# B's rows copied to four blocks of 32 partitions, B spread by 32-row matmuls, and one projection bank for two batches in a Mamba kernel

## The chip, the cores and the metric

The kernel runs on one core of a Trainium2 chip. The metric is the time of one execution on the device in microseconds (us); of several executions the median is taken. TensorE is called PE, VectorE DVE, ScalarE ACT, GpSimd POOL and the queue that issues most DMAs SP, as in the profile.

## What is computed

Four layers run one after the other on x of shape (4, 96, 64, 64). Layers 0 and 2 are the same block with two Mamba sublayers each; layer 1 is a state-space layer of another kind, and layer 3 a ConvNeXt block. Only layers 0 and 2 are touched. One Mamba sublayer, cut to what matters:

```
h   = layernorm(seq)                          # (B, L=4096, C=96)
xs, z = split(h @ in_w)                       # 192 channels each
xc  = silu(causal_conv4(xs) + conv_b)
dbl = xc @ xproj_w                            # 6 + 16 + 16 columns
dt, Bm, Cm = dbl[:6], dbl[6:22], dbl[22:38]
delta = softplus(dt @ dt_w + dt_b)            # 192 channels
dA  = exp(delta * A)                          # 192 channels x 16 states
dBx = delta * Bm * xc
hs[t] = dA[t] * hs[t-1] + dBx[t]              # a scan over L
y   = (sum over states of hs * Cm + D * xc) * silu(z)
seq = seq + y @ out_w
```

Bm and Cm are the same for all 192 channels, so each of their rows has to be brought to every channel's partition.

## The kernel before, in words

The activations X stay on chip as 96 partitions x 4 batches x 4096 positions. `mamba_fusion` runs a Mamba layer in 32 steps: 2 pairs of batches x 2 sublayers x 8 tiles of T = 512 positions. In a step both batches of a pair are worked on: 2 x 192 channels fill three tiles j of 128 partitions (`SEGS`): j = 0 holds 128 channels of the first batch, j = 1 the last 64 of the first batch and the first 64 of the second, j = 2 the other 128 of the second. Two layers make 64 steps.

A step has a front and a scan. `mamba_front` (L141) is a generator: layernorm of both batches, the projections pu (with the convolution folded in, L165) and pz (L173), a SiLU on ACT between two loads of its function table, then pd (L189), which is `xproj` and gives dt, a row of ones (added by the bias `one7`), B and C as 39 rows for each batch. Each batch has its own pd bank and eviction into `dbl[b]` (L193), and C is written to DRAM from there (L194). Then pt (L202) makes delta from 7 rows of `dbl`, and ACT, DVE and POOL finish the softplus (delta, du).

`mamba_scan` (L214) walks through 24 groups of GS = 2 states (8 groups for each j). For a group it does the following. `spread` multiplies a selector `sel` with `dbl[b]` on PE, which puts B's row s on all partitions of a two-bank PSUM tile bs (L232); the selector and `dbl` have 128 rows, of which one counts. A DMA brings C's rows to all partitions (cs, L259). ACT makes da (L262, recorded at L96). DVE multiplies bs by du (L263) and runs two scans (L268). POOL multiplies hs by cs (L269), and PE sums over states with an identity (py, L246). The spread of group n + 1 is issued before the scans of group n, the sums of group n - 1 after them. bs has two buffers, so spread n + 1 waits until the scans of group n - 1 have read theirs.

The next step's front is woven in by hand: after each group one `next()` takes one more piece of the front, up to its next `yield`. There are 15 pieces, so groups 0 to 14 of a step have front work behind them and the later ones don't. The order on each engine comes from the framework's scheduler, which follows this program order but may let ready work pass. In j = 1 a spread has two matmuls of 64 columns for each state, one for each batch.

Of the kernel before, what the change touches and what calls it, by code (L numbers as in the profile page):

```python
# [16 lines left out]
F32 = mybir.dt.float32  # L17
AF = mybir.ActivationFunctionType
ALU = mybir.AluOpType
# [6 lines left out]
P = 128  # L26
T = 512
# [6 lines left out]
DIN = 192  # L34
NST = 16
RANK = 6
NXP = RANK + 1 + 2 * NST
GS = 2


# [97 lines left out]
    nc.gpsimd.tensor_tensor(relu, relu, w, ALU.add)  # L138


def mamba_front(tc, k, X, pools, wt, pair, c, h2, dbl4, made):  # L141

    nc = tc.nc
    work, psum, dram = pools
    h, hprev = h2[c % 2], h2[(c + 1) % 2]
    if c == 0:
        nc.vector.memset(h[:C, :, 0:3], 0.0)
    else:
        nc.vector.tensor_copy(h[:C, :, 0:3], hprev[:C, :, T : T + 3])
    for b in range(2):  # L150
        layernorm(
            nc, k, (work, psum), X[:, 2 * pair + b, ds(c * T, T)], h[:C, b, 3 : 3 + T],
            wt["ln"][:, 0:1], wt["ln"][:, 1:2], tag="mm",
        )
        yield

    xz = made["xz"] = work.tile([P, 6, T], F32, name="xz", bufs=2)
    for j in range(3):  # L160
        pu = psum.tile([P, T], F32, tag="mm", name="pu")
        for r0, r1, d0, d1, b in SEGS[j]:
            for tap in range(4):
                kk = C + 1 if tap == 3 else C
                nc.tensor.matmul(  # L165
                    pu[r0:r1], lhsT=wt["conv"][:kk, tap, d0:d1], rhs=h[:kk, b, ds(tap, T)],
                    start=(tap == 0), stop=(tap == 3),
                )
            yield
        nc.scalar.copy(xz[:, j], pu)  # L170
        pz = psum.tile([P, T], F32, tag="mm", name="pz")
        for r0, r1, d0, d1, b in SEGS[j]:
            nc.tensor.matmul(  # L173
                pz[r0:r1], lhsT=wt["in"][:, DIN + d0 : DIN + d1], rhs=h[:C, b, 3 : 3 + T],
                start=True, stop=True,
            )
        nc.scalar.copy(xz[:, 3 + j], pz)
        yield
    k.act.other(xz, xz, AF.Silu)
    yield  # L180

    cd = made["cd"] = dram.tile([2, NST, T], F32, name="cd")
    dbl = made["dbl"] = dbl4[c % 2]
    for b in range(2):
        pd = psum.tile([P, T], F32, tag="mm", name="pd")[:NXP]
        for n, (j, r0, r1) in enumerate(ROWS[b]):
            nc.tensor.matmul(  # L189
                pd, lhsT=wt["xproj"][r0:r1, j], rhs=xz[r0:r1, j], start=(n == 0), stop=(n == 1)  # L190
            )
        db = dbl[b]
        nc.scalar.activation(db[:NXP], pd, AF.Identity, bias=wt["one"])  # L193
        nc.sync.dma_start(cd[b], db[RANK + 1 + NST : NXP])  # L194
        yield

    delta = made["delta"] = work.tile([P, 3, T], F32, name="delta", bufs=2)
    du = made["du"] = work.tile([P, 3, T], F32, name="du", bufs=2)
    for j in range(3):
        pt = psum.tile([P, T], F32, tag="mm", name="pt")  # L200
        for r0, r1, d0, d1, b in SEGS[j]:
            nc.tensor.matmul(  # L202
                pt[r0:r1], lhsT=wt["dt"][:, d0:d1], rhs=dbl[b][: RANK + 1], start=True, stop=True
            )
        ua = work.tile([P, T], F32, name="ua")
        lg = work.tile([P, T], F32, name="lg")
        nc.scalar.activation(ua, pt, AF.Abs)
        nc.vector.tensor_scalar_max(delta[:, j], pt, 0.0)
        softplus_tail(nc, k.act, delta[:, j], ua, lg, du[:, j])
        nc.gpsimd.tensor_tensor(du[:, j], delta[:, j], xz[:, j], ALU.mult)  # L210
        yield


def mamba_scan(tc, k, X, pools, wt, sel, pair, c, carry, made, fuse):  # L214

    nc = tc.nc
    state, psum = pools
    xz, cd, dbl, delta, du = made["xz"], made["cd"], made["dbl"], made["delta"], made["du"]
    groups = [(j, s0) for j in range(3) for s0 in range(0, NST, GS)]

    def spread(n):

        j, s0 = groups[n]
        bs = psum.tile([P, GS, T], F32, tag="bs", name="bs", bufs=2)
        for s in range(GS):  # L230
            for r0, r1, _, _, b in SEGS[j]:
                nc.tensor.matmul(  # L232
                    bs[r0:r1, s], lhsT=sel[:, s0 + s, r0:r1], rhs=dbl[b], start=True, stop=True
                )
        return bs

    def close(j, py):
        nc.vector.scalar_tensor_tensor(
            xz[:, j], xz[:, j], wt["d"][:, j : j + 1], py, ALU.mult, ALU.add
        )  # L240
        nc.gpsimd.tensor_tensor(xz[:, j], xz[:, j], xz[:, 3 + j], ALU.mult)

    def sums(n, py, hc):
        j, s0 = groups[n]
        for s in range(GS):
            nc.tensor.matmul(  # L246
                py, lhsT=k.ident, rhs=hc[:, s], start=(s0 + s == 0), stop=(s0 + s == NST - 1)
            )
        if s0 + GS == NST:
            close(j, py)  # L250

    bs = spread(0)
    last = None
    for n, (j, s0) in enumerate(groups):
        if s0 == 0:
            py = psum.tile([P, T], F32, tag="py", name="py", bufs=2)
        cs = state.tile([P, GS, T], F32, name="cs", bufs=4)
        for r0, r1, _, _, b in SEGS[j]:
            nc.sync.dma_start(cs[r0:r1], cd[b, s0 : s0 + GS, :].partition_broadcast(r1 - r0))  # L259
        da = state.tile([P, GS, T], F32, name="da", bufs=3)  # L260
        for s in range(GS):
            k.act.exp_ln(da[:, s], delta[:, j], AF.Exp, scale=wt["a"][:, j, s0 + s : s0 + s + 1])  # L262
        nc.vector.tensor_tensor(bs, bs, du[:, j : j + 1].to_broadcast([P, GS, T]), ALU.mult)  # L263
        ahead = spread(n + 1) if n + 1 < len(groups) else None
        hs = state.tile([P, GS, T], F32, name="hs", bufs=3)
        for s in range(GS):
            init = 0.0 if c == 0 else carry[:, j, s0 + s : s0 + s + 1]
            nc.vector.tensor_tensor_scan(hs[:, s], da[:, s], bs[:, s], init, ALU.mult, ALU.add)  # L268
        nc.gpsimd.tensor_tensor(cs, hs, cs, ALU.mult)  # L269
        if c < NT - 1:  # L270
            nc.scalar.copy(carry[:, j, s0 : s0 + GS], hs[:, :, T - 1])  # L271
        if last is not None:
            sums(*last)
        last = (n, py, cs)
        bs = ahead
        yield
    sums(*last)

    for b in range(2):
        po = psum.tile([P, T], F32, tag="mm", name="po")[:C]  # L280
        for n, (j, r0, r1) in enumerate(ROWS[b]):
            nc.tensor.matmul(
                po, lhsT=wt["out"][r0:r1, j], rhs=xz[r0:r1, j], start=(n == 0), stop=(n == 1)
            )
        xs = X[:, 2 * pair + b, ds(c * T, T)]
        nc.vector.tensor_tensor(xs, xs, po, ALU.add)
        fuse(2 * pair + b, c)


def mamba_weights(nc, act, wpool, w, sub, one7):  # L290
    wt = {"one": one7}
    for name, shape in (
        ("ln", [C, 2]), ("in", [C, 2 * DIN]), ("xproj", [P, 3, NXP]), ("dt", [RANK + 1, DIN]),
        ("a", [P, 3, NST]), ("d", [P, 3]), ("out", [P, 3, C]),
    ):
        wt[name] = wpool.tile(shape, F32, name=f"w_{name}{sub}")
        nc.sync.dma_start(wt[name], w[name][sub])
    conv = wt["conv"] = wpool.tile([C + 1, 4, DIN], F32, name=f"w_conv{sub}")
    nc.sync.dma_start(conv[:C], w["conv_wT"][sub].partition_broadcast(C))
    nc.sync.dma_start(conv[C : C + 1, 3], w["conv_b"][sub : sub + 1])  # L300
# [9 lines left out]
def mamba_fusion(ctx: ExitStack, tc, k, X, res, w):  # L310
# [17 lines left out]
    for b in range(B):  # L328
# [7 lines left out]
    gb = one.tile([C, B], F32, name="gb")  # L336
    nc.scalar.activation(gb, pg2, AF.Identity, bias=vec[:, 1:2])

    one7 = one.tile([NXP, 1], F32, name="one7")
    nc.gpsimd.memset(one7, 0.0)  # L340
    nc.gpsimd.affine_select(
        out=one7, in_=one7, compare_op=ALU.not_equal, fill=1.0, base=-RANK,
        pattern=[[0, 1]], channel_multiplier=1,
    )
    h2 = [one.tile([C + 1, 2, T + 3], F32, name=f"h{i}") for i in range(2)]
    for h in h2:
        nc.vector.memset(h[C : C + 1], 1.0)

    sel = one.tile([P, NST, P], F32, name="sel")
    nc.gpsimd.memset(sel, 0.0)  # L350
    nc.gpsimd.affine_select(
        out=sel, in_=sel, compare_op=ALU.not_equal, fill=1.0, base=-(RANK + 1),
        pattern=[[-1, NST], [0, P]], channel_multiplier=1,
    )
    dbl4 = [[one.tile([P, T], F32, name=f"dbl{i}{b}") for b in range(2)] for i in range(2)]
    for db in dbl4[0] + dbl4[1]:
        nc.gpsimd.memset(db, 0.0)
    stats = one.tile([C, B * NT, nc.vector.BN_STATS_DIM], F32, name="stats")

    def fuse(b, c):  # L360
# [10 lines left out]
    def front(n, made):  # L371
        if n < len(steps):
            pair, sub, c = steps[n]
            yield from mamba_front(tc, k, X, (work, psum, dram), wts[sub], pair, c, h2, dbl4, made)


    made = {}
# [565 lines left out]
```

## Time and profile before

| what | value |
|---|---|
| median of 3 runs | 13629.11 us (13625.45 to 13630.94) |
| profiled execution, its own time | 13637.25 us |
| its span in the profile | 13635.5 us |
| mean granted PE clock | 0.978 |
| L232 spread, PE records | 8192, 3031.1 us busy |
| L246 sums over states, PE records | 6144, 2994.9 us busy |
| L268 scans, DVE | 2688 with a carry, 3304.5 us busy |
| L263 bs times du, DVE | 1536, 1873.7 us busy |
| L269 hs times cs, POOL | 1536, 3620.2 us busy |

An fp32 matmul leaves two records on PE, each with its weight load on PEld. Busy times are unions of spans, and the spans of neighbouring PE records overlap, so PE is read best by the distance from one start to the next. In an answer in order of time the columns are the start, the length, the engine, the line, the operation, output and inputs, rows * columns of the array, shapes, the count of merged instructions, and in brackets the idle time before with what ended it. Of the chain of work that ended last, 60% of the span lies on PE and 24% on DVE.

### The profile page before, as it was taken

To read this page: it belongs to the slowest core of one execution; us is meant where nothing else is said; L and a number is where in the kernel's file an instruction comes from. 1 tells how busy PE (TensorE), PEld (TensorE's weight loads), DVE (VectorE), ACT (ScalarE), POOL (GpSimd) and SP (SyncE) were. 2 spreads that over 40 slices of the span, in tenths; PEclk is the share of its full clock that TensorE was granted. 3 is DMA by queue.
4 is the path that set the end of the run, shared out by engine and by line. 5 is a ranking of instruction groups with operands and counts; after the bars stand their busy time and mean duration, and the time that the engine had idled before them with its cause. 6 is when DMAs were issued, how large, how long until landed. Compare 5 with 4: busy or idle time off the path is not lost.

```text
span 13635.5 us, 125211 instructions
## 1 busy us (share of the span) xinstructions
PE 12543.4 (92%) x43016; PEld 5819.2 (43%) x43016; DVE 9062.4 (66%) x11224; ACT 5552.3 (41%) x9606; POOL 6819.1 (50%) x4814
## 2 busy tenths in 40 slices
PE   8999999999997999999999999899999999999887
PEld 2333333333334666666666666333333333333232
DVE  6777777777775444444444444677777777777798
ACT  3444444344443444444444444444444434444233
POOL 4555555555553444444444344555555555555344
PEclk9999999999998999999999999999999999999887
DMA  3333333333332000000000000233333333333100
GB/s 104 95 98 100 95 98 98 98 101 95 98 99 60 1 1 5 1 1 5 1 1 1 5 1 1 90 95 99 100 94 99 97 98 101 97 98 100 57 8 9
DMA packets 248125, 853.46 MB, mean 63 GB/s; under 512 B 40065, under 2 KB 41345, under 8 KB 246722
## 3 DMA queue, kind: packets, MB, share of 16 engines
q1 hardware_dynamic: 247490, 845.47, 20.4%
q8 instruction: 341, 5.59, 0.2%
q14 instruction: 294, 2.41, 0.1%
HBM read 828.54 MB, written 16.78 MB: 62 GB/s over the span
## 4 chain that ended last, share of the span: by engine, by line
PE 60%; DVE 24%; issue 6%; POOL 6%; ACT 4%; DMA 1%; DVEq 0%; POOLq 0%; SPq 0%; ACTq 0%
DVE hs L268 14%; PE front L558 14%; PE bs L232 11%; PE py L246 10%; PE pu L165 7%; DVE bs L263 6%; PE att L603 2%; PE y L640 2%; POOL y L837 2%; PE y L644 2%; PE out L680 1%; PE out L684 1%; POOL cs L269 1%; PE pz L173 1%; DVE acc L811 1%
## 5 line engine op out<-in xcount | busy, mean ns | idle before, releaser
L269 POOL TENSOR_TENSOR cs<-hs,cs 128x1024 f32<-128x1024 f32 x1536 | 3620.2, 2358 | 2948.9 <-DVE hs L268 2125.6
L246 PE MATMUL py<-cs,ident 128*128 128x512 f32 x6144 | 2994.9, 610 | 426.0 <-POOL cs L269 420.3
L268 DVE TENSOR_TENSOR_SCAN hs<-da,carry,bs 128x512 f32<-128x512 f32 x2688 | 3304.5, 1266 | 123.5 <-ACT da L96 2.4
L232 PE MATMUL bs<-dbl,sel 128*128 128x512 f32 (+1 forms) x8192 | 3031.1, 603 | 141.9 <-DVE hs L268 141.9
L263 DVE TENSOR_TENSOR bs<-bs,du 128x1024 f32<-128x1024 f32 x1536 | 1873.7, 1220 | 1233.3 <-PE bs L232 1233.2
L96 ACT ACTIVATE da<-delta,w_a 128x512 f32<-128x512 f32 x3072 | 2053.9, 712 | 314.8 <-DVE hs L268 312.5
L246 PEld LDWEIGHTS py<-cs,ident 128*128 128x128 f32 x6144 | 1078.7, 189 | 2234.4 <-issue 1201.0
L232 PEld LDWEIGHTS bs<-dbl,sel 128*128 128x128 f32 (+1 forms) x8192 | 1022.9, 163 | 1930.8 <-issue 1532.4
L558 PE MATMUL front<-sconv,xn 96*128 96x320 f32 (+1 forms) x4096 | 1215.5, 436 | 4.7 <-DVE pre L570 4.7
L271 ACT COPY carry<-hs 128x2 f32<-128x2 f32 x1344 | 257.6, 192 | 2174.1 <-DVE hs L268 2174.0
L626 POOL TENSOR_TENSOR ce<-ce,pre 128x384 f32<-128x384 f32 x496 | 509.5, 1027 | 974.9 <-ACT ce L96 974.1
L610 DVE TENSOR_SCALAR seg<-att,dac 128x128 f32<-128x128 f32 x1536 | 452.6, 343 | 744.7 <-PE att L607 733.6
L165 PE MATMUL pu<-h,w_conv 96*128 96x512 f32 (+3 forms) x2048 | 934.9, 601 | 6.8 <-ACT rs L96 1.7
L558 PE MATMUL front<-xn,sconv 96*128 96x512 f32 (+1 forms) x2048 | 929.8, 592 | 0.0
L618 DVE SCALAR_TENSOR_TENSOR seg<-cb,dt,seg 128x128 f32<-128x128 f32 x1536 | 805.9, 578 | 163.1 <-ACT seg L96 161.4
L558 PEld LDWEIGHTS front<-sconv,xn 96*128 96x128 f32 (+1 forms) x4096 | 743.0, 191 | 253.2 <-issue 12.6
L811 DVE SCALAR_TENSOR_TENSOR acc<-pad,c_conv,acc 96x1024 f32<-96x1024 f32 x560 | 707.9, 1331 | 26.3 <-issue 25.1
L96 ACT ACTIVATE seg<-seg 128x384 f32<-128x384 f32 x512 | 266.5, 522 | 854.6 <-DVE seg L610 818.1
L621 POOL TENSOR_TENSOR seg<-seg,skip 128x384 f32<-128x384 f32 x512 | 511.6, 999 | 162.9 <-DVE seg L618 151.9
L165 PEld LDWEIGHTS pu<-h,w_conv 96*128 96x128 f32 (+3 forms) x2048 | 320.0, 164 | 595.5 <-issue 549.9
L696 POOL TENSOR_TENSOR X<-X,rs 96x256 f32<-96x256 f32 x256 | 210.8, 823 | 680.2 <-DVE rs L689 680.2
L640 PE MATMUL y<-seg,pre 128*64 128x128 f32 x3072 | 430.3, 291 | 127.5 <-POOL seg L621 126.6
(173 smaller groups left out, 14691.3 us busy)
## 6 DMA issues: line engine op xcount, KB each, us to landing
cs<-cd SPq DMA_DIRECT2D x1024, 512.0 KB, 3.7
cs<-cd SPq DMA_DIRECT2D x1024, 256.0 KB, 3.9
X<-in_x SPq DMA_DIRECT2D x4, 1536.0 KB
r<-in_x SPq DMA_DIRECT2D x16, 384.0 KB, 3.6
res<-X SPq DMA_DIRECT2D x4, 1536.0 KB, 7.8
r<-res SPq DMA_DIRECT2D x16, 384.0 KB, 3.5
out<-y SPq DMA_DIRECT2D x32, 192.0 KB, 2.1
cd<-dbl SPq DMA_DIRECT2D x128, 32.0 KB, 2.1
```

Of the source, the lines that this page charges most:

```text
L96: self._behind(self.scalar.activation(out, in_, func, **kw), self.loaded)
L165: nc.tensor.matmul(pu[r0:r1], lhsT=wt["conv"][:kk, tap, d0:d1], rhs=h[:kk, b, ds(tap, T)], start=(tap == 0), stop=(tap == 3),)
L232: nc.tensor.matmul(bs[r0:r1, s], lhsT=sel[:, s0 + s, r0:r1], rhs=dbl[b], start=True, stop=True)
L246: nc.tensor.matmul(py, lhsT=k.ident, rhs=hc[:, s], start=(s0 + s == 0), stop=(s0 + s == NST - 1))
L263: nc.vector.tensor_tensor(bs, bs, du[:, j : j + 1].to_broadcast([P, GS, T]), ALU.mult)
L268: nc.vector.tensor_tensor_scan(hs[:, s], da[:, s], bs[:, s], init, ALU.mult, ALU.add)
L269: nc.gpsimd.tensor_tensor(cs, hs, cs, ALU.mult)
L558: nc.tensor.matmul(out, lhsT=lhsT, rhs=rhs, start=(tap == 0), stop=(tap == 3))
L618: nc.vector.scalar_tensor_tensor(seg[:, h], cb, made["dt"][:, col : col + 1], seg[:, h], ALU.mult, ALU.mult)
L621: nc.gpsimd.tensor_tensor(seg, seg, self.skip, ALU.add)
L640: nc.tensor.matmul(py[rows, cols], lhsT=xb[:, ch], rhs=seg[:, h], start=True, stop=first)
L811: nc.vector.scalar_tensor_tensor(acc, window(n, 0, rows, tap), wt["conv"][:, tap : tap + 1], acc, ALU.mult, ALU.add)
```

## The change

`NXP` becomes 32 and now is the height of one block of rows. The weights of `xproj` are laid out anew in SBUF, in 64 columns: for q = 0 and 1 a block of 32 with dt's 6 columns, an empty one, B's 16 and half of C's (8), and one column of zeros. The projection pd then gives, for each batch, two blocks of 32 rows, both with dt, the ones and B. Both batches go into one PSUM bank, the first on partitions 0 to 63, the second on 64 to 127, with the halves of the contraction ordered so that both batches' 128-row parts come first and the 64-row parts follow. One eviction moves all 128 partitions into `dbl`, now a tile of the work pool with two buffers; C leaves in four DMAs of 8 rows. The front has one yield fewer there.

The spread takes 32 rows of `sel` and `dbl` for a matmul: state s of a group uses block s of the batch. `sel` holds its pattern on all four blocks (four selects at the start in place of one), `one7` has its one in each block, and the four `dbl` tiles with their memsets are gone. `dt`'s weights are loaded twice, to partitions 0 to 6 and 64 to 70[...].

```diff
--- before.py
+++ after.py
@@ -34,7 +34,10 @@
 DIN = 192
 NST = 16
 RANK = 6
-NXP = RANK + 1 + 2 * NST
+
+
+NXP = 32
+CROW = RANK + 1 + NST
 GS = 2
 
 
@@ -138,7 +141,7 @@
     nc.gpsimd.tensor_tensor(relu, relu, w, ALU.add)
 
 
-def mamba_front(tc, k, X, pools, wt, pair, c, h2, dbl4, made):
+def mamba_front(tc, k, X, pools, wt, pair, c, h2, made):
 
     nc = tc.nc
     work, psum, dram = pools
@@ -182,17 +185,21 @@
 
 
     cd = made["cd"] = dram.tile([2, NST, T], F32, name="cd")
-    dbl = made["dbl"] = dbl4[c % 2]
+    dbl = made["dbl"] = work.tile([P, T], F32, name="dbl", bufs=2)
+    pd = psum.tile([P, T], F32, tag="mm", name="pd")
+    for n in range(2):
+        for b in range(2):
+            j, r0, r1 = ROWS[b][n if b == 0 else 1 - n]
+            nc.tensor.matmul(
+                pd[2 * NXP * b : 2 * NXP * (b + 1)], lhsT=wt["xproj"][r0:r1, j], rhs=xz[r0:r1, j],
+                start=(n == 0), stop=(n == 1),
+            )
+    nc.scalar.activation(dbl, pd, AF.Identity, bias=wt["one"])
     for b in range(2):
-        pd = psum.tile([P, T], F32, tag="mm", name="pd")[:NXP]
-        for n, (j, r0, r1) in enumerate(ROWS[b]):
-            nc.tensor.matmul(
-                pd, lhsT=wt["xproj"][r0:r1, j], rhs=xz[r0:r1, j], start=(n == 0), stop=(n == 1)
-            )
-        db = dbl[b]
-        nc.scalar.activation(db[:NXP], pd, AF.Identity, bias=wt["one"])
-        nc.sync.dma_start(cd[b], db[RANK + 1 + NST : NXP])
-        yield
+        for q in range(2):
+            r = NXP * (2 * b + q) + CROW
+            nc.sync.dma_start(cd[b, q * NST // 2 : (q + 1) * NST // 2], dbl[r : r + NST // 2])
+    yield
 
     delta = made["delta"] = work.tile([P, 3, T], F32, name="delta", bufs=2)
     du = made["du"] = work.tile([P, 3, T], F32, name="du", bufs=2)
@@ -200,7 +207,8 @@
         pt = psum.tile([P, T], F32, tag="mm", name="pt")
         for r0, r1, d0, d1, b in SEGS[j]:
             nc.tensor.matmul(
-                pt[r0:r1], lhsT=wt["dt"][:, d0:d1], rhs=dbl[b][: RANK + 1], start=True, stop=True
+                pt[r0:r1], lhsT=wt["dt"][2 * NXP * b : 2 * NXP * b + RANK + 1, d0:d1],
+                rhs=dbl[2 * NXP * b : 2 * NXP * b + RANK + 1], start=True, stop=True,
             )
         ua = work.tile([P, T], F32, name="ua")
         lg = work.tile([P, T], F32, name="lg")
@@ -229,8 +237,10 @@
         bs = psum.tile([P, GS, T], F32, tag="bs", name="bs", bufs=2)
         for s in range(GS):
             for r0, r1, _, _, b in SEGS[j]:
+                rows = ds(NXP * (2 * b + s), NXP)
                 nc.tensor.matmul(
-                    bs[r0:r1, s], lhsT=sel[:, s0 + s, r0:r1], rhs=dbl[b], start=True, stop=True
+                    bs[r0:r1, s], lhsT=sel[rows, s0 + s, r0:r1], rhs=dbl[rows],
+                    start=True, stop=True,
                 )
         return bs
 
@@ -290,11 +300,22 @@
 def mamba_weights(nc, act, wpool, w, sub, one7):
     wt = {"one": one7}
     for name, shape in (
-        ("ln", [C, 2]), ("in", [C, 2 * DIN]), ("xproj", [P, 3, NXP]), ("dt", [RANK + 1, DIN]),
+        ("ln", [C, 2]), ("in", [C, 2 * DIN]),
         ("a", [P, 3, NST]), ("d", [P, 3]), ("out", [P, 3, C]),
     ):
         wt[name] = wpool.tile(shape, F32, name=f"w_{name}{sub}")
         nc.sync.dma_start(wt[name], w[name][sub])
+    xp = wt["xproj"] = wpool.tile([P, 3, 2 * NXP], F32, name=f"w_xproj{sub}")
+    nc.vector.memset(xp, 0.0)
+    for q in range(2):
+        nc.sync.dma_start(xp[:, :, NXP * q : NXP * q + CROW], w["xproj"][sub, :, :, :CROW])
+        nc.sync.dma_start(
+            xp[:, :, NXP * q + CROW : NXP * q + CROW + NST // 2],
+            w["xproj"][sub, :, :, CROW + q * NST // 2 : CROW + (q + 1) * NST // 2],
+        )
+    wt["dt"] = wpool.tile([2 * NXP + RANK + 1, DIN], F32, name=f"w_dt{sub}")
+    for b in range(2):
+        nc.sync.dma_start(wt["dt"][2 * NXP * b : 2 * NXP * b + RANK + 1], w["dt"][sub])
     conv = wt["conv"] = wpool.tile([C + 1, 4, DIN], F32, name=f"w_conv{sub}")
     nc.sync.dma_start(conv[:C], w["conv_wT"][sub].partition_broadcast(C))
     nc.sync.dma_start(conv[C : C + 1, 3], w["conv_b"][sub : sub + 1])
@@ -336,25 +357,24 @@
     gb = one.tile([C, B], F32, name="gb")
     nc.scalar.activation(gb, pg2, AF.Identity, bias=vec[:, 1:2])
 
-    one7 = one.tile([NXP, 1], F32, name="one7")
+    one7 = one.tile([P, 1], F32, name="one7")
     nc.gpsimd.memset(one7, 0.0)
-    nc.gpsimd.affine_select(
-        out=one7, in_=one7, compare_op=ALU.not_equal, fill=1.0, base=-RANK,
-        pattern=[[0, 1]], channel_multiplier=1,
-    )
+    for q in range(P // NXP):
+        nc.gpsimd.affine_select(
+            out=one7, in_=one7, compare_op=ALU.not_equal, fill=1.0, base=-(NXP * q + RANK),
+            pattern=[[0, 1]], channel_multiplier=1,
+        )
     h2 = [one.tile([C + 1, 2, T + 3], F32, name=f"h{i}") for i in range(2)]
     for h in h2:
         nc.vector.memset(h[C : C + 1], 1.0)
 
     sel = one.tile([P, NST, P], F32, name="sel")
     nc.gpsimd.memset(sel, 0.0)
-    nc.gpsimd.affine_select(
-        out=sel, in_=sel, compare_op=ALU.not_equal, fill=1.0, base=-(RANK + 1),
-        pattern=[[-1, NST], [0, P]], channel_multiplier=1,
-    )
-    dbl4 = [[one.tile([P, T], F32, name=f"dbl{i}{b}") for b in range(2)] for i in range(2)]
-    for db in dbl4[0] + dbl4[1]:
-        nc.gpsimd.memset(db, 0.0)
+    for q in range(P // NXP):
+        nc.gpsimd.affine_select(
+            out=sel, in_=sel, compare_op=ALU.not_equal, fill=1.0, base=-(NXP * q + RANK + 1),
+            pattern=[[-1, NST], [0, P]], channel_multiplier=1,
+        )
     stats = one.tile([C, B * NT, nc.vector.BN_STATS_DIM], F32, name="stats")
 
     def fuse(b, c):
@@ -371,7 +391,7 @@
     def front(n, made):
         if n < len(steps):
             pair, sub, c = steps[n]
-            yield from mamba_front(tc, k, X, (work, psum, dram), wts[sub], pair, c, h2, dbl4, made)
+            yield from mamba_front(tc, k, X, (work, psum, dram), wts[sub], pair, c, h2, made)
 
 
     made = {}
```

## The prediction

> **What bounds the kernel now.** I read the page first (busy shares, slices), then who waits for whom, then busy time in two stretches of one scan step, then TensorE, VectorE and ScalarE in order of time inside such a step.
>
> ```profile
> PE 12543.4 (92%) x43016; PEld 5819.2 (43%) x43016; DVE 9062.4 (66%) x11224; ACT 5552.3 (41%) x9606; POOL 6819.1 (50%) x4814
> PE   8999999999997999999999999899999999999887
> DVE  6777777777775444444444444677777777777798
> ```
>
> The change touches the two Mamba layers only: slices 1 to 12 and 26 to 37, where PE is 9 tenths busy and DVE 7. But which of the two ends last changes inside a step.
>
> ```profile
> DVE bs L263 <- PE bs L232: 1233.2, 748, 3.6
> 477.00:556.00 79.00, 78.34 (x208) 26.83 (x207) 57.54 (x51) 37.52 (x68) 41.68 (x22) 1.00 0.33 93
> 560.00:590.00 30.00, 24.10 (x53) 9.30 (x52) 29.01 (x24) 10.71 (x23) 23.49 (x12) 1.00 0.34 119
> ```
>
> First the wait: VectorE sits 1233 us in all waiting for the spread of B (L232), 19 us in each of the 64 steps. Then two stretches of the step from 473 to 602 us (columns: length, then busy us and instructions of PE, PEld, DVE, ACT, POOL, then clock). While the next step's front is woven in (477 to 556) PE is busy 78.3 of 79.0 us and DVE has 21.5 us idle: PE is the bound. Without front (560 to 590) DVE is busy 29.0 of 30.0 us: there a group of two states costs VectorE 1.2 + 2.45 us, and a faster spread brings nothing.
>
> ```profile
> 1005.62 1.88 PE L232 MATMUL bs<-dbl,sel 128*128 128x512 f32 x4
> 1007.34 1.88 PE L246 MATMUL py<-cs,ident 128*128 128x512 f32 x4
> 1009.06 1.02 PE L173 MATMUL pz<-h,w_in 96*128 96x512 f32 x2
> ...
> 1042.46 1.98 PE L246 MATMUL py<-cs,ident 128*128 128x512 f32 x4
> 1044.37 1.94 PE L232 MATMUL bs<-dbl,sel 128*64 128x512 f32 x8
> 1046.24 1.98 PE L246 MATMUL py<-cs,ident 128*128 128x512 f32 x4
> ...
> 1054.50 1.60 PE L189 MATMUL pd<-xz,w_xproj 64*39 64x512 f32 x3
> ...
> 1058.18 1.98 PE L246 MATMUL py<-cs,ident 128*128 128x512 f32 x4
> 1060.10 1.12 PE L202 MATMUL pt<-dbl,w_dt 7*128 7x512 f32 x2
> 1061.15 1.94 PE L232 MATMUL bs<-dbl,sel 128*64 128x512 f32 x8
> ...
> 1064.93 1.07 PE L202 MATMUL pt<-dbl,w_dt 7*64 7x512 f32 x4
> 1065.93 1.94 PE L232 MATMUL bs<-dbl,sel 128*64 128x512 f32 x8
> ...
> 1112.26 1.10 PE L282 MATMUL po<-xz,w_out 64*96 64x512 f32 x4
> ```
>
> Read the distance of starts (busy spans overlap). An fp32 matmul leaves two records. Full-width: four records 1.72 us (1005.62 to 1007.34), 0.43 each. A PE that changes the shape of its tiles pays: py between two changes takes 1.91 (1042.46 to 1044.37), 0.19 more. Side by side works in both directions already: eight 64-column records take 1.87 (1044.37 to 1046.24), little over half of 8 x 0.43; and the four records of po on rows 0 to 63 and 64 to 127, in two banks, end within 1.10 us. A short run of one tile shape costs 1.05 for two passes of 128 columns (pt, 1060.10) and 1.00 for two passes of 2 x 64 columns (1064.93).
>
> ```profile
> 475.85 1.12 PE L232 MATMUL bs<-dbl,sel 128*128 128x512 f32 x2 [1.33 <-DVE hs L268]
> 476.81 1.02 PE L123 MATMUL pv<-sq,mean 96*96 96x512 f32 x2
> 477.67 1.02 PE L232 MATMUL bs<-dbl,sel 128*128 128x512 f32 x2
> ...
> 524.94 1.28 ACT L100 ACT_TABLE_LOAD   x1
> ...
> 530.38 2.56 ACT L96 ACTIVATE da<-delta,w_a 128x512 f32<-128x512 f32 x4
> ```
>
> Two things the sum needs: spreads 2 and 3 of a step stand in halves around pv, and SiLU with its two table loads holds ScalarE for 5.4 us, so that da, and the scan behind it, come no earlier than 530.38.
>
> [...] Trace: po agrees for two groups of 64 rows; nothing shows groups of 32, or four tiles at once. [...] bs[:, 0] and bs[:, 1] are two banks. In j=1 two row tiles share a bank, but in other partitions.
>
> **The change part by part** (groups n = 0 to 23 of a step, spreads s0 to s23; j = 0, 1, 2 by eights).
>
> *Spread, one batch* (j = 0, 2). Now 4 x 0.43 = 1.72 us. After: two row groups side by side, two passes, as pt: 1.05; but py beside it goes from 1.72 to 1.91. Saved: 0.48. For s6 and s7, which follow 64-column pu and pay the way in already: 1.83 - 1.05 - 0.10 = 0.68.
>
> *Spread, both batches* (j = 1). Now 1.87. After: four tiles of 32 x 64, if all run together two passes, as pt 7*64: 1.00. Saved 0.87; s8, which today follows 64-column pz without a change of shape, 0.73. If only pairs run together, nothing.
>
> *Projection pd.* Now 1.96 us in one group and, from 1054.50 to 1058.18 less a spread of 1.87, 1.81 in the next. After: both batches beside each other in two column tiles, one 128-row pair and one 64-row pair, 2 x 1.00 = 2.0 in one group. Saved 1.8, all in the second. One eviction of 128 partitions in place of two (0.68 us of ACT, hidden). Two DMAs more on SP are some 0.65 us of issue each (two took 1.29 us at 74.78 us); queued behind them are the cs fetches, four buffers ahead of their use, so it is hidden; without that cover 1.3 us a step. pt now waits for one eviction of both batches; behind pt on PE stands the next spread, but an order of some 3 us of PE work (a spread and py) lies between pd and pt, against 0.7 us of eviction: nothing, and 0.7 at most. The front has one yield fewer, so pt and the softplus pieces on ACT, DVE and POOL run one group earlier, where VectorE is the bound before and after: nothing.
>
> *What a step gains*, in order, against 473 to 602 us:
> - s2, s3 in halves: each half now changes shape in and out for 0.39 (twice 0.19), with nothing beside it. Three halves lie in the saturated part: -1.2. If they stand together instead: +1.0.
> - s4 to s8: 2 x 0.48 + 2 x 0.68 + 0.73 = 3.0. The shortest of these chunks of PE stays at 3.8 us, over VectorE's 3.7, so all counts.
> - s9 to the SiLU: SiLU follows pz, which follows s9. s9 is 0.87 shorter, and mult(11), which today stands before scan(10) because spread 11 comes late, gets out of its way (530.38 to 531.19, 0.8). +1.7. The shorter s10 and s11 are worth nothing: late next is da behind SiLU.
> - After SiLU: VectorE waited 2.30 us for s13 (second pd before it) and 0.43 for s14. With 1.00 + 1.91 + 1.05 us of PE per group, about 4.0, and scan(11) done at the same time, some 0.3 is left. +2.4.
> - From there VectorE is the bound until the last scan: 0.
> - First spread of the next step, in front of an idle VectorE: 1.9 to 1.2: +0.7.
>
> Sum: 3.0 + 1.7 + 2.4 + 0.7 - 1.2 = 6.6 us. Two of 64 steps have no front: 62 x 6.6 = 409 us.
>
> *Setup.* Three more selects on sel (2.0 us each on POOL by the trace) against four memsets of 1.9 us less: nothing. Four strided xproj DMAs per set behind a memset that queues after the sums on DVE: they stand ahead of conv on SP, estimated 0 to 10 us for a layer; I take 4, so 8.
>
> 13,637 us for the profiled execution (span 13,635.5) - 409 + 8 = 13,236; that execution is 8 us over the median of the runs, so 13,230.
>
> **Rivals.**
> - *Pairs only* (0.10): two row groups overlap but four tiles don't. The j = 1 terms go (0.73, 0.87, some 1.3 after SiLU): 3.7 us a step, 13,410. For it: no four tiles in the trace. Against: two by rows and two by columns both run at full rate.
> - *Halves stay whole* (0.15): s2 and s3 aren't split, 8.8 us a step, 13,090.
> - *Slower: the two halves of a spread don't run together* (0.20), because other work is ordered between them everywhere, as now in s2 and s3, or because 32-row groups don't overlap. A split one-batch spread costs 2 x (0.86 + 0.39) - 1.72 = +0.78, a two-batch one some +0.3. All of them: 7 x 0.78 + 8 x 0.3 + 0.3 - 1.8 for pd = +6.4 us a step, 14,030. Each spread that falls so turns a gain of 0.5 to 0.9 into a loss of 0.3 to 0.8; with more than about six of the fifteen in the saturated part it is slower. Without overlap but unsplit only the 0.39 is paid: +1 us a step, 13,690. For it: order around pv; 32-row groups not seen. Against: all other spreads stand whole in the trace.
> - *No change* (0.05): VectorE late wherever PE gets faster, or setup eats it. Against: 21.5 us of idle VectorE.
> - *Clock*: more idle on PE could lower the grant[...]. No own chance.
>
> **Numbers.** Forecast 0.50, halves whole 0.15, pairs only 0.10, no change 0.05, slower 0.20. Predicted 13,230. The range starts at 13,080 and ends at 13,690, the mild end of the slower case; the likeliest one's own range is 13,100 to 13,420. A change of 0.2% (27 us) is what a measurement can tell. Faster 0.75, same 0.05, slower 0.20.
>
> **What would show it.** Right: in the changed trace the one-batch bs has pairs of records starting within some 10 ns and a length of 1.05 from start to start, the two-batch one 1.00; py beside them 1.91; DVE bs <- PE bs falls from 1233 to some 800 us; a step takes some 123 in place of 129.8 us; the SiLU gap stays. Wrong: starts 0.43 apart, bs in halves in most groups, more PE busy time a step than now, or a clock under 1.00 between 477 and 556.

## The result, and the profile after

| | before | changed |
|---|---|---|
| median of 4 runs | 13630.03 us | 13676.49 us (13670.61 to 13692.86) |
| ratio, 95% interval | | 1.0036 [1.0019, 1.0053] |
| span of the profiled execution | 13635.5 us | 13673.4 us |
| mean granted PE clock | 0.978 | 0.929 |

The kernel became 0.36% slower; 13,230 was forecast. The page of the changed kernel, its lines for PE, VectorE and the granted clock:

```profile
PE 12143.5 (89%) x43016; PEld 5378.4 (39%) x43016; DVE 9081.2 (66%) x11228; ACT 5505.6 (40%) x9542; POOL 6789.9 (50%) x4818
...
PE   7888988888887999999999999888898888888787
...
PEclk8999999999998999999999999899998999999897
```

The clock's line of the kernel before, to set beside the last one:

```profile
PEclk9999999999998999999999999999999999999887
```

PE is busy 400 us less than before, and still the end comes later. Slices 1, 26 and 31 of the clock, inside the Mamba layers, read 8 where they read 9 before. First, though, whether the new instructions have the lengths that the sum gave them. PE of the changed kernel in order of time, in the step from 475 to 605 us (start, length, engine, line, operation, count, idle before):

```profile
474.06 1.10 PE L122 MATMUL pc<-X,center 96*96 96x512 f32 x2
477.19 2.07 PE L241 MATMUL bs<-dbl,sel 32*128 32x512 f32 x2 [2.03 <-DVE hs L278]
479.19 2.02 PE L126 MATMUL pv<-sq,mean 96*96 96x512 f32 x2
481.14 2.07 PE L241 MATMUL bs<-dbl,sel 32*128 32x512 f32 x2
483.15 3.78 PE L256 MATMUL py<-cs,ident 128*128 128x512 f32 x4
...
488.00 1.12 PE L241 MATMUL bs<-dbl,sel 32*128 32x512 f32 x2
489.06 1.10 PE L126 MATMUL pv<-sq,mean 96*96 96x512 f32 x2
...
496.49 1.13 PE L241 MATMUL bs<-dbl,sel 32*128 32x512 f32 x4
497.54 1.98 PE L256 MATMUL py<-cs,ident 128*128 128x512 f32 x4
...
527.56 1.09 PE L241 MATMUL bs<-dbl,sel 32*64 32x512 f32 x8
528.58 1.99 PE L256 MATMUL py<-cs,ident 128*128 128x512 f32 x4
530.50 1.09 PE L241 MATMUL bs<-dbl,sel 32*64 32x512 f32 x8
```

They have: a one-batch spread takes 1.05 us from start to start (496.49 to 497.54), a two-batch one, four tiles at once, 1.02 (527.56 to 528.58), and py beside them 1.92 (528.58 to 530.50). But between 477 and 487 us every matmul is twice as long: py spans 3.78 us there and 1.98 later, a half of a spread 2.07 and 1.12. The table by stretches says why (length; busy us and instructions of PE, PEld, DVE, ACT, POOL; then the granted clock). The changed kernel:

```profile
473.70:477.10 3.40, 1.46 (x5) 0.24 (x2) 3.27 (x4) 0.59 (x1) 0.00 (x0) 1.00 0.00 0
477.10:487.40 10.30, 10.21 (x11) 3.13 (x12) 7.76 (x8) 4.06 (x8) 5.47 (x3) 0.50 0.00 0
487.40:556.00 68.60, 63.41 (x198) 20.12 (x198) 50.14 (x45) 33.99 (x61) 37.29 (x20) 1.00 0.34 102
...
559.00:562.50 3.50, 3.17 (x4) 1.17 (x4) 3.50 (x4) 0.28 (x2) 3.34 (x4) 0.51 0.00 0
```

The same places of the kernel before:

```profile
473.50:489.30 15.80, 14.36 (x34) 5.59 (x33) 14.17 (x14) 8.00 (x15) 8.62 (x5) 1.00 0.17 66
556.00:569.00 13.00, 8.37 (x19) 2.93 (x18) 12.70 (x11) 5.05 (x10) 12.69 (x9) 1.00 0.24 87
```

The grant is halved for 10.2 us around spreads 2 and 3 and for shorter stretches behind spreads 16 and 17. The prediction had named a clock under 1.00 between 477 and 556 us as a sign of being wrong; it read 1.00 there before, and now:

```profile
477.00:556.00 79.00, 73.61 (x208) 23.25 (x210) 58.00 (x52) 38.05 (x69) 42.76 (x23) 0.94 0.30 88
```

Call the 60 steps that are neither the first nor the last of a layer the middle steps. All 60 lose the grant both in groups 0 to 3 and in groups 14 to 18. Half clock adds up to 1338 us in them, and to 7 us in the kernel before. (Wherever a sum of half clock is given from here on, it is over the middle steps, from a step's first scan to the next step's.) Where the time of a step went is read from the start of one group's first scan to the next group's; these are means over the middle steps, in us:

| groups | before | changed | change | forecast of the change |
|---|---|---|---|---|
| 1 to 3 | 15.44 | 20.01 | +4.6 | +0.7 (halves +1.2, spread 4 -0.5) |
| 4 to 8 | 30.49 | 27.35 | -3.1 | -2.5 without spread 9 |
| 9 to 11 (SiLU) | 14.28 | 14.26 | 0.0 | -1.7 with spread 9 |
| 12 to 15 (pd, pt) | 25.19 | 22.97 | -2.2 | -2.4 |
| 17 and 18 | 8.08 | 10.00 | +1.9 | 0 |
| 23 (the next step's first spread) | 13.90 | 13.75 | -0.2 | -0.7 |
| whole step | 129.79 | 130.78 | +1.0 | -6.6 |

Groups 4 to 15 gained 5.4 of the 6.6 us that the sum gave them; groups 1 to 3, 17 and 18 gave it all back and more. (In these profiles the two Mamba layers became 57 us longer. The rest of the program, which isn't touched, took 18 us less, within the 28 us over which it ranges in the ten traces.)

### The profile page after: what moved, and what is told of

Same layout as the page of the kernel before. It is cut to its first block, busy times and chain, and to the rows that moved or that the text cites. A ratio compares the mean times of both kernels' runs of the same rounds, so it can differ in the third digit from the quotient of the medians.

```text
span 13673.4 us, 125311 instructions
## 1 busy us (share of the span) xinstructions
PE 12143.5 (89%) x43016; PEld 5378.4 (39%) x43016; DVE 9081.2 (66%) x11228; ACT 5505.6 (40%) x9542; POOL 6789.9 (50%) x4818
## 3 DMA queue, kind: packets, MB, share of 16 engines
q14 instruction: 295, 2.42, 0.1%
## 4 chain that ended last, share of the span: by engine, by line
PE 57%; DVE 23%; ACT 7%; issue 6%; POOL 5%; DMA 1%; DVEq 0%; POOLq 0%; SPq 0%; ACTq 0%
DVE hs L278 14%; PE front L578 14%; PE py L256 12%; PE bs L241 7%; PE pu L168 7%; DVE bs L273 5%; PE att L623 2%; PE y L660 2%; PE y L664 2%; PE out L700 1%; PE out L704 1%; PE pv L126 1%; ACT xz L103 1%; PE pz L176 1%; POOL cs L279 1%
## 5 line engine op out<-in xcount | busy, mean ns | idle before, releaser
L256 PE MATMUL py<-cs,ident 128*128 128x512 f32 x6144 | 3472.3, 693 | 778.7 <-POOL cs L279 778.6
L273 DVE TENSOR_TENSOR bs<-bs,du 128x1024 f32<-128x1024 f32 x1536 | 1872.4, 1219 | 1119.0 <-PE bs L241 1100.4
L256 PEld LDWEIGHTS py<-cs,ident 128*128 128x128 f32 x6144 | 1164.1, 210 | 2990.4 <-POOL cs L279 1535.4
L241 PE MATMUL bs<-dbl,sel 32*128 32x512 f32 (+1 forms) x8192 | 2060.8, 651 | 233.2 <-DVE hs L278 233.2
L241 PEld LDWEIGHTS bs<-dbl,sel 32*128 32x128 f32 (+1 forms) x8192 | 506.0, 163 | 1677.6 <-issue 1112.1
```

The costliest lines, as they stand in the source:

```text
L241: nc.tensor.matmul(bs[r0:r1, s], lhsT=sel[rows, s0 + s, r0:r1], rhs=dbl[rows], start=True, stop=True,)
L256: nc.tensor.matmul(py, lhsT=k.ident, rhs=hc[:, s], start=(s0 + s == 0), stop=(s0 + s == NST - 1))
```

## The experiments

Theories on record, none of them shown by the two traces so far. A: the grant goes with how many of the array's rows are at work over a stretch of time, so that 32-row tiles bring little. B: it goes with idle time alone. C: the clock is beside the point, and the halves of spreads 2 and 3 with their changes of shape cost the time. Versions e1, e2, e3, e5 and e6 ran once each, e4, e7 and e8 four times.

**e1: fill the gap with full-height work.** In the changed kernel, with `fill` = 2 for the first batch of a step and 0 for the second:

```diff
+    for _ in range(fill):
+        nc.tensor.matmul(pc, lhsT=k.center, rhs=src, start=True, stop=True)
     nc.tensor.matmul(pc, lhsT=k.center, rhs=src, start=True, stop=True)
```

> The changed kernel, with two more 96-row matmuls of the first batch's mean removal (pc, written twice over with the same values) in each step, in the gap in which PE waits before the second spread (2.0 us idle at 475.2 to 477.2). Clock theory (A: the grant counts how many of the array's rows work; B: it counts idle time alone): the grant stays at 1.00 from 477 to 487, groups 1 to 3 of a step lose 3.6 us of the 4.4 us that they had gained, a step is about 126.9 us, the whole 13,450. Order theory (C: the halves of spreads 2 and 3 and their changes of shape cost the time): nothing comes back, 13,670 to 13,700.

Measured: 13574.18 us in one run (before 13628.45), half clock 925 us. Work that nobody needs made the kernel 102 us faster than the changed one, which C excludes; but that is under half of what A and B had named. The stretches of e1 show why:

```profile
601.70:604.70 3.00, 2.85 (x8) 0.90 (x6) 2.87 (x3) 0.00 (x0) 0.00 (x0) 1.00 0.00 0
604.70:608.10 3.40, 2.42 (x5) 0.81 (x6) 3.27 (x4) 1.91 (x4) 2.35 (x1) 1.00 0.00 0
608.10:614.90 6.80, 6.80 (x8) 1.77 (x7) 4.69 (x5) 2.52 (x5) 3.63 (x3) 0.50 0.02 10
```

The filled stretch keeps its grant. The next one, in which a half of spread 2 runs on 32 rows and PE is busy 2.42 of 3.40 us, loses it all the same. The expectation had taken the gap for the only cause.

The same trace separates the clock from the halves. In 26 of its 60 middle steps the grant holds through groups 0 to 3, in 34 it falls there. Groups 1 to 3 take 16.5 us in the 26 and 19.0 in the 34, with spreads 2 and 3 in halves in both. So the halves alone don't make the 20.0 us of the changed kernel.

**e2: the same filler on 32 rows.**

```diff
+        nc.tensor.matmul(pc, lhsT=k.center[:32], rhs=src[:32], start=True, stop=True)
```

> The same filler with the same busy time, but on 32 rows of the array only. A: a window of 3.4 us with this gap then has about 0.38 of its rows-times-time at work, against some 0.40 below which the trace shows drops; the grant still falls at 477 in most steps, 13,640 to 13,700. B: same as with the 96-row filler, 13,450. C: nothing comes back, 13,670 to 13,700, with the grant as it may be.

Measured: 13851.03 us, half clock 1642 us; slower than without filler by 175 us, and above the 13,700 that A had named. No middle step keeps the grant in groups 0 to 3, where 26 did in e1. The filler is as long as in e1 and has a third of its rows, and the grant falls after a stretch in which PE was busy 3.13 of 3.45 us:

```profile
615.30:618.75 3.45, 3.13 (x7) 0.70 (x5) 3.45 (x3) 1.02 (x3) 0.82 (x1) 1.00 0.00 0
618.75:629.00 10.25, 9.43 (x11) 2.63 (x10) 6.70 (x7) 3.41 (x7) 5.48 (x4) 0.50 0.01 6
```

B falls with this pair.

**e3: spreads 0 to 3 on 128 rows.**

```diff
+                if n < 4:
+                    nc.tensor.matmul(
+                        bs[r0:r1, s], lhsT=wsel[:, b, s0 + s, r0:r1], rhs=dbl, start=True, stop=True
+                    )
+                    continue
                 rows = ds(NXP * (2 * b + s), NXP)
```

> The changed kernel with spreads 0 to 3 of a step on all 128 rows again (a second selector with one block of ones); all else as changed. A and B: the grant holds at 477, groups 1 to 3 are back at the 13.4 us of before (4.08, 5.78, 5.54, of which 0.5 for spread 4 is gained), -4.8 us a step, 13,380; the drops near 559 and 566, behind spreads 16 and 17, stay. C: the same groups come back only by 1.2 us, 13,600.

Measured: 13380.76 us. Groups 1 to 3 take 4.08, 5.78 and 4.89 us; no half clock is left in groups 0 to 3, and 505 us of it are stretches that begin in group 14, which ends behind spread 16. This alone doesn't decide against C, since spreads on 128 rows have no change of shape at pv either; e1 does.

**e4: 128 rows for spreads 16 to 19 too.** The condition of e3 becomes `n < 4 or 16 <= n < 20`.

> Spreads 0 to 3 and 16 to 19 on all 128 rows, 4 to 15 and 20 to 23 in 32-row tiles, pd as changed. A and B: no drop of the grant inside a step, mean clock of the Mamba layers as before; gains of spreads 4 to 9 (3.1 us) and after the SiLU (2.4 us) stay, groups 17 and 18 are back (1.7 us less than the changed kernel), so some 6 us a step under before: 13,260, ratio to before 0.973. C: about 13,550.

Measured: 13281.36 us, ratio to before 0.9747 [0.973, 0.9763]: faster than both kernels. The page's clock, and the wait that had been 1233.2 us before and is 1100.4 in the changed kernel:

```profile
PEclk9999999999998999999999999999999999999887
```

```profile
DVE bs L278 <- PE bs L246: 643.8, 324, 3.0
```

Half clock is down to 89 us. Group 17 is back at 4.37 us. Spread 2 of e4 stands in halves like the changed kernel's, with a gap before it, and keeps its speed (e4, in order of time):

```profile
458.00 1.12 PE L241 MATMUL bs<-dbl,wsel 128*128 128x512 f32 x2 [1.33 <-DVE hs L283]
458.96 1.02 PE L126 MATMUL pv<-sq,mean 96*96 96x512 f32 x2
459.83 1.02 PE L241 MATMUL bs<-dbl,wsel 128*128 128x512 f32 x2
460.69 1.88 PE L261 MATMUL py<-cs,ident 128*128 128x512 f32 x4
```

**e5: the projection alone**, every spread on 128 rows.

```diff
-                rows = ds(NXP * (2 * b + s), NXP)
                 nc.tensor.matmul(
-                    bs[r0:r1, s], lhsT=sel[rows, s0 + s, r0:r1], rhs=dbl[rows],
+                    bs[r0:r1, s], lhsT=sel[:, b, s0 + s, r0:r1], rhs=dbl,
```

> One part alone: both batches' projection in one bank and one dbl as in the changed kernel, but every spread on all 128 rows (selectors with a single block of ones). Row-share theory of the clock (A): no 32-row tiles but pt, so the grant stays as before (mean about 0.977), and only the 1.8 us of the second pd chunk and part of the wait behind it come back, about 2 us a step: 13,505. If instead the merged projection moved the clock or cost something, it is at or above 13,630.

Measured: 13500.86 us against 13633.32, 2.1 us less per step, clock 0.979. Of e4's gain of 347 us, 132 are the projection's, so some 215 are the tiles', if the two simply add.

**e6: the halves together.** pc and pv of each batch become pieces of their own, with a `yield` after the square, so that the scheduler lets both halves of a spread pass.

```diff
         nc.scalar.activation(sq, pc, AF.Square)
+        yield
         pv = psum.tile([P, T], F32, tag="mm", name="pv")[:C]
```

> The changed kernel with the layernorm's two matmuls (pc, pv) in two pieces of the front each, so that the two halves of spreads 2 and 3 stand together. A: the gap of 2 us before spread 2 stays, so the grant still falls there, but the busy rows behind it are more and it comes back in one or two windows of 3.4 us in place of three; half-clock time in groups 0 to 3 is 200 to 400 us in place of 560, groups 1 to 3 take 16 to 18 us in place of 19.8; the drop behind spreads 16 and 17 stays; 13,500 to 13,620. Order theory (C): the halves were all of it; groups 1 to 3 return to some 13 us, 13,260, whatever the grant does.

Measured: 13629.93 us, half clock 1512 us. Both halves stand together, and the grant is still lost:

```profile
479.90 1.13 PE L247 MATMUL bs<-dbl,sel 32*128 32x512 f32 x4 [2.03 <-DVE hs L284]
482.49 3.78 PE L262 MATMUL py<-cs,ident 128*128 128x512 f32 x4 [1.46 <-POOL cs L285]
486.06 1.91 PE L161 MATMUL pv<-sq,mean 96*96 96x512 f32 x2
```

Groups 1 to 3 read 13.3 us, which is C's figure, but the front's pieces moved two groups on, so this can't be set against the other kernels. Half clock in groups 0 to 3 was 389 us, inside A's range, while A's total of 13,620 was missed by 10 us: more of it than in the changed kernel lies in groups 13 and 16 to 19. C's 13,260 is off by 370.

**e7 and e8: two more versions.** e7 has 128 rows in spreads 20 to 22 too (the condition for 128 rows is `n < 4 or 16 <= n < 23`, and the selectors are cut to the columns that they need); e8 is e4 with spread 0 back in 32-row tiles (`1 <= n < 4 or 16 <= n < 20`).

> As e4, but spreads 20 to 22 are on all 128 rows too (only 4 to 15 and 23 in 32-row tiles). These spreads are bound by DVE, so tiles bring nothing there, and A has the remaining drops at the step's end (102 us of half clock in group 23 in e4) go: 13,250 to 13,281, ratio 0.972 to 0.975. If that half-clock time cost nothing: 13,281.

> As e4, but with spread 0 in 32-row tiles again, which stands in front of an idle DVE: 0.65 us a step less by the length of the spread (13,240, ratio 0.9715). A warns that the share of working rows around the step's start falls with it: if the grant falls at group 0 in most steps, it is above e4's 13,281.

Measured: e7 13285.22 us, ratio 0.9744 [0.973, 0.9759], half clock 102 us against e4's 89: no gain. The "102 us of half clock in group 23 in e4", on which its expectation rests, are a misreading. 99 of them are one stretch behind the last step of the first Mamba layer, which the kernel before has as well (first line before, second e4):

```profile
4214.30:4313.20 98.90, 35.82 (x94) 21.01 (x95) 32.63 (x54) 35.72 (x50) 16.79 (x14) 0.50 0.25 67
4043.00:4141.90 98.90, 37.11 (x96) 21.90 (x97) 32.27 (x52) 35.22 (x48) 16.77 (x14) 0.50 0.25 67
```

There was nothing at the step's end to bring back; e7 shows only that 128 rows cost nothing that can be seen in spreads 20 to 22. e8 13301.69 us, ratio 0.9755 [0.9739, 0.9772]: group 23 is shorter as expected in the steps of the first sublayer (12.82 us for 13.47), but longer in the second's (14.66 for 14.30; more on this below). The stretches of half clock that begin in group 11 rose to 171 us (51 in e4), and group 12 takes 6.17 us in place of 4.66 (medians). The expectation looked for it at group 0. The edit didn't touch groups 11 and 12. Perhaps the windows of the count below came to lie otherwise over the step; that was neither tried nor shown.

**A count over all ten traces.** No trace shows what sets the grant; what stood before each of its drops can be counted. All changes of the grant lie on a grid of 3.413 us. For each window of this grid at full clock between the first and the last scan of a Mamba layer I added up, from the trace's PE records, rows / 128 over each record's time (from its start to 0.165 us before its end, since neighbours overlap by 0.163 us in the median, in the kernel before and in the changed one). Rows were rounded up to a multiple of 32, a choice of this count, and summed where records run together, never over 1. The windows by this share, and how many were followed by a halved grant:

```
share of rows x time   grant halved   grant kept
under 0.36                      767            0
0.36 to 0.40                    110           31
0.40 to 0.44                     72          159
0.44 to 0.50                      5         1002
0.50 and more                     0        19551
```

Split at 0.41, this share misplaces 98 of 21,697 windows. The split is taken from the same windows that it is tried on; one at 0.40, taken from the changed kernel's trace alone, misplaces 98 of the 19,684 windows of the nine others. Busy time alone misplaces 315 at its best split: 250 of the 954 drops came from windows in which PE was busy for half the time or more, 27 of them for 0.9 or more, while 721 windows with PE busy for less than half kept the grant. Rows times columns misplaces 254: a two-batch spread fills only half the array's area, but all its rows, and the grant reads 1.00 in the stretch with these spreads (487.40 to 556.00 us of the changed kernel). These are counts in one program; that rows are what the grant depends on, they don't show.

## Why the prediction was wrong, point by point

- *Spread of one and of two batches, py beside them:* right. 1.05, 1.02 and 1.92 us were measured for 1.05, 1.00 and 1.91. Two 32-row groups and four tiles run together, so neither "pairs only" nor the overlap half of the slower rival came true.
- *pd:* right. Alone it brought 2.1 us a step for 1.8 and part of the wait behind it (e5).
- *s4 to s8, and after the SiLU:* right. Groups 4 to 8 became 3.1 us shorter, of which 0.85 are spread 9's; groups 12 to 15 became 2.2 shorter for 2.4.
- *SiLU:* mis-sized; 1.7 us were forecast and 0.85 came, in group 8. The 0.8 us by which mult(11) was to get out of scan(10)'s way wasn't there to gain. In the changed kernel da starts at 533.71 and takes 0.7 us, and the scan starts at 534.52, 0.81 after da's start, with mult(11) long done. Before, it started 0.81 after da's start too (530.38 to 531.19). mult(11) had stood beside da, not in front of the scan. Before, then changed:

```profile
531.19 1.28 DVE L268 TENSOR_TENSOR_SCAN hs<-da,carry,bs 128x512 f32<-128x512 f32 x1
```

```profile
533.71 1.34 ACT L99 ACTIVATE da<-delta,w_a 128x512 f32<-128x512 f32 x2
```

```profile
534.52 2.45 DVE L278 TENSOR_TENSOR_SCAN hs<-da,carry,bs 128x512 f32<-128x512 f32 x2 [1.64 <-ACT da L99]
```

- *First spread of a step:* right in the steps of the first sublayer (medians of group 23: 13.47 to 12.83 us). In the second sublayer's steps group 23 became longer (14.30 to 14.66), at full clock. There spread 0 stands in halves around a matmul that the prediction left out, the fusion's pf, in both kernels. The half that took 0.96 us from start to start (1503.85 to 1504.81) takes 1.05 on 32 rows (1513.13 to 1514.18), and the next matmuls take longer too: pf 1.03 for 0.96, po 2.05 for 1.96, the second pf 1.03 for 0.91.
- *Setup:* 8 us estimated; the first scan starts 1.1 us earlier than before (85.9 for 87.0), so nothing.
- *The step that failed: the clock, whose cost was put at nothing.* "No own chance." The forecast took the grant for a matter of long idle gaps on PE and found none long enough in its sums; how long a gap has to be was not shown by the trace of the kernel before. In the changed kernel 3.40 us with a gap of 2.03 us, 1.46 us of PE work and, counted as above, a share of 0.24 stood before the drop to 0.50 (473.70 to 477.10 us). Busy time doesn't settle it either, since e2 lost the grant after 3.13 us of 3.45. Half speed then met spreads 2 and 3, where PE is the bound (busy 10.21 of 10.30 us). Of the 7.6 us between the forecast (-6.6 a step) and what came (+1.0), 3.9 lie in groups 1 to 3, 1.9 in groups 17 and 18, 1.1 in groups 4 to 11 (mostly the SiLU), 0.5 in the first spread and 0.2 after the SiLU. Of the 3.9, at least 3.5 are the clock's: 20.0 us against the 16.5 of e1's steps that kept the grant. The rest, up to 0.4, is what the halves cost over the 1.2 that they were given. The 1.9 are the clock's as well, since e4, with spreads 16 to 19 on 128 rows, has them back.
- *The slower rival*, given 0.20, met the time nearly (13,690 for its mild end) with a mechanism that didn't happen; that the time lies inside the stated range is luck. The order around pv, which spoke for it, has a part of its own: at full clock groups 1 to 3 take 16.5 us with the halves on 32 rows (e1's 26 steps) and 14.8 on 128 rows (e3). So the halves cost 1.8 us at most, as the filler of e1 also holds pv back:

```profile
606.80 1.10 PE L128 MATMUL pv<-sq,mean 96*96 96x512 f32 x2 [0.82 <-ACT sq L126]
```

Shown: the loss is tied to the rows of spreads 0 to 3 and 16 to 19 (e3, e4), most of it comes with the grant and not with the halves (e1), and idle time alone doesn't explain the grant (e1 against e2). Only counted from traces, not tried by itself: that columns don't matter. Not told apart: rows at work and the amount of data streamed into them, which change together in every version. Open: what decides between 0.36 and 0.44, and what brings the grant back.

## What to carry to other kernels

In this kernel matmuls on fewer rows saved time where PE was the bound and dense (3.1 us a step in groups 4 to 8); beside a gap a window came down to a share of 0.24, and the grant read 0.50 in the next. In a kernel like this one, use row tiles in the saturated part of a loop, and leave full-height matmuls, even wasteful ones, next to waits: e4 does that, and 0.9747 came of it in place of 1.0036. In a forecast for it, set up the rows-times-time of every 3.413 us window around each gap before and after, not the gap alone. The kernel before was nearer to the shares at which drops were counted than its clock of 1.00 tells: at the start of the step at 473 us its window around the gap before spread 2 had a share of 0.50, and 5 of the 1007 windows from 0.44 to 0.50 were followed by one.

## What the runs showed of the hardware

- In this program's ten traces the granted clock went with the share of rows at work in windows of 3.413 us: halved after all 767 windows under 0.36, after none of 19,551 at 0.50 and over.
- Two 32-row tiles into two banks ran side by side: four records in 1.05 us from start to start, where four of 128 x 128 took 1.72. Four 32 x 64 tiles did too, two of them at a time writing one bank, on different partitions: eight records in 1.02 us, where eight of 128 x 64 took 1.87.
- A filler that computes nothing of use made a kernel faster by 102 us on 96 rows and slower by 175 us on 32.
